# A sparse graph kernel whose gathered edge values are replaced by diagonal values, with a pass that counts them

## The chip, the cores and the metric

The kernel runs on one core of one Trainium2 chip. The metric is the device time of one execution in microseconds (us), taken without a profiler. The engines are TensorE (PE in the profile; its weight loads are PEld), VectorE (DVE), ScalarE (ACT), GpSimd (POOL) and SyncE (SP), which here only issues DMAs. Each engine works through its own queue in order, and semaphores order the engines against each other. SBUF is the memory on the chip that the engines work in, PSUM holds the sums of TensorE.

## The reference, cut to what matters

There are N = 2708 nodes with D = 128 features. `adj` is a random sparse 0/1 matrix with ones on the diagonal whose rows are divided by their sums, so all nonzero values of one row are equal, and equal to the row's diagonal element.

```python
# layer 0
XW = mobius_matvec(W, X)
gamma = 2.0 / maximum(1.0 - sum(XW * XW), EPS)
two_mean = (A_hat @ (gamma * XW)) / _clamp_abs(A_hat @ (gamma - 1.0))
...
x = layernorm(x + expmap0(relu(logmap0(AXW))))
# layer 1
s = x @ msg_w[:, :D].T
d = x @ msg_w[:, D:].T
messages = gelu(s[:, None, :] + d[None, :, :] + msg_b)
aggregated = einsum('ijd,ij->id', messages, adj)
h = gelu(concat([x, aggregated]) @ upd_w.T + upd_b) + x
x = layernorm(x + (layernorm(h) * ln_w + ln_b))
```

Layer 0 is a dense product of `adj` with a 128-column matrix. Layer 1 needs a message only where `adj[i, j]` is not zero, which is a few edges per node.

## The kernel before, in words

The nodes stand in NB = 22 blocks of 128 rows. The host hands over `adj` itself, its transpose in blocks without the diagonal (`adj_t`), and a packed array with the weights and the diagonal, `dg[:, b]` for block b.

**Layer 0.** After a setup (lines up to 310) that makes the 130 columns of `y`, the main loop walks over the blocks. `layer0(b)` loads the block's part of `adj_t` (128 × 22 × 128 float32, 1.44 MB) through SP into `aT`, which has two buffers (L317). ScalarE turns it into signs in bfloat16 (`sgn`, one buffer, L319), which also sums them per row into `signs`. TensorE multiplies it with `y` in 22 matmuls (L324), and VectorE adds the diagonal part (L328).

**Finding the edges.** From the signs, `keys` makes rows of keys on TensorE (L350), from which VectorE takes the largest eight at a time (MAX8, L358). `extract(l)` turns a list of these into tiles of 128 edges each. There are 25 lists and 99 tiles (TILES), where a tile t holds 128 edges of one block: `R[:, t, :]` says as a 0/1 matrix which row each edge belongs to (L412, L414), `J[:, t]` holds the index of the neighbour (L447), and `rid[:, t]` the number of the row (L444). They come out of matmuls with `R` (L438) and a nearest distance (L441). The address of the edge's element in `adj` is then made in `F` (L448, three buffers, one per list), and POOL fetches the value itself with an indirect DMA, one for each tile, into `V[:, t]` (the `gather` of L191). Lists found in one block are finished in the next two, interleaved with their layer-0 matmuls. The small tiles of `extract` come from a pool with two buffers per name.

**Between the layers.** `layer0_end` runs for the blocks 0–15 during the main loop and for 16–21 after it. It finishes layer 0, makes `s` (`s_nm`) and `d`, and writes `d` through SP to a table in DRAM (L535), from which the messages' gathers read.

**Layer 1.** First ScalarE applies Gelu to the sum of s and d of each node itself (L583), the message along the diagonal, and multiplies it with the diagonal (L585, 22 instructions); `own` adds it to the block's sum on TensorE (L669). Then `messages` walks over a block's tiles in quads of up to four: POOL gathers the rows d_j of 128 edges (L191), TensorE multiplies `R` with `s_nm` (L652) to lay s_i beside them, VectorE makes the weighted 0/1 matrix `rv` for the way back (L654) and adds both (L657), ScalarE applies Gelu (L658), and TensorE sums the messages per row into the PSUM tile `ag` (L660). The gathered rows go into a ring of RING = 7 quads, and later into a freed `aT` buffer, the slab. For the first EARLY = 8 blocks the edges to nodes below 16 × 128 are done ahead in a loop of their own (L687, result copied at L691); then the loop over GROUPS of blocks does the rest, copies the sum to `agT` (L702), and calls `update` (four or five matmuls and a Gelu, L606–L614) and, per group, `finish` (two layer norms and the output's DMA through SP, L616–L637). There are 35 quads in all.

**The end.** L708–L757 sum several conditions under which the lists of edges could be incomplete into one flag, among them whether the sum of the signs equals the number of edges found. The flag is read at L759; if it is set, a dense form of layer 1 follows (L760). With this input it is not.

The order in each engine's queue is made by a planner from the program's order, its dependencies and its own costs, so that instructions of neighbouring quads interleave; `issue_after` and `high_priority` bind it at the borders of the stages.

Of the kernel before, what the change touches and what calls it, by code (L numbers as in the profile page):

```python
# [31 lines left out]


SPLIT = 16
RING = 7


# [38 lines left out]
def hyperbolic_then_message_kernel(  # L76
# [4 lines left out]
    x_nm: bass.AP,  # L81
    x_t: bass.AP,
    pack: bass.AP,
    table: bass.AP,
# [22 lines left out]
    w0_sb, wT, rowvec, o = pk[:, :D], pk[:, D : 5 * D].rearrange("p (i d) -> p i d", d=D), {}, 5 * D  # L107
# [3 lines left out]
    mb, dg = pk[:, o : o + 1], pk[:, o + 1 : o + 1 + NB]  # L111
# [14 lines left out]
    ones_b = const.tile([P, P], BF16, name="ones_b")  # L126
# [39 lines left out]

    R = big.tile([P, NT, P], F32, name="R")
    J = const.tile([P, NT], U32, name="J")
    V = const.tile([P, NT], F32, name="V")
    rid = const.tile([P, NT], F32, name="rid")  # L170
    top = const.tile([P, NC], F32, name="top")
    limit = const.tile([P, NT], F32, name="limit")
# [17 lines left out]
    def gather(o, src, at):  # L190
        nc.gpsimd.indirect_dma_start(  # L191
            out=o, out_offset=None, in_=src, in_offset=bass.IndirectOffsetOnAxis(ap=at, axis=0)
        )
# [5 lines left out]
    def bank(name, bufs=2):  # L199
        return ps.tile([P, 512], F32, name=name, bufs=bufs)  # L200
# [10 lines left out]

    def cols(n):
        count[0] += 1
        return sc.tile([P, n], F32, name=f"c{count[0]}")

    def rsqrt(v, n, pool=None):

# [94 lines left out]
    ss, ssp = cols(NB), cols(NB)  # L312

    def layer0(b):

# [50 lines left out]
    def extract(l):  # L366
# [2 lines left out]
        C = wa + wb  # L369

        def tmp(name, dt=F32, w=CMAX):
            return small.tile([P, w], dt, name=name)[:, :C]

        tk = top[:, c0 : c0 + C]
        u0, u1 = 8 * (wa > 0), C - 8 * (wb > 0)
# [51 lines left out]
            )  # L427
        z = zs[l % 2][:, : C + 1]
        nc.vector.scalar_tensor_tensor(z[:, 1:], scan, SPAN, code, op0=OP.mult, op1=OP.add)
        F = small.tile([P, TMAX], U32, name="F", bufs=3)  # L430
        step = 512 // (C + 1)
        for k0 in range(0, n, step):
            k1 = min(n, k0 + step)
            w = k1 - k0
            t = slice(t0 + k0, t0 + k1)
            sp = bank("sel", 1)[:, : w * (C + 1)].rearrange("p (t c) -> p t c", t=w)
            for k in range(w):
                nc.tensor.matmul(sp[:, k, :], lhsT=R[:, t0 + k0 + k, :], rhs=z, start=True, stop=True)  # L438

            dist = small.tile([P, 512], F32, name="work", bufs=3)[:, : w * C].rearrange("p (t c) -> p t c", t=w)  # L440
            nc.vector.tensor_tensor(  # L441
                dist, sp[:, :, 1:], place[:, k0:k1].unsqueeze(2).to_broadcast([P, w, C]), op=OP.subtract
            )
# [4 lines left out]
            nc.vector.scalar_tensor_tensor(  # L448
                F[:, k0:k1], J[:, t], float(b * P * N - 1), rid[:, t], op0=OP.add, op1=OP.add
            )  # L450
        for t in range(t0, t0 + n):
            gather(V[:, t : t + 1], adj.rearrange("i (j o) -> (i j) o", o=1), F[:, t - t0 : t - t0 + 1])

    x1, x1T = x_sb, xT
    s_nm = mx
# [1 line left out]
    def layer0_end(b0, b1):  # L457

        n = b1 - b0
        sb = slice(b0, b1)  # L460

        den, r = nom[:, sb, D], nom[:, sb, D + 1]
        di, t, v, e, f = (cols(n) for _ in range(5))
# [112 lines left out]

    gd = nom
    for ins in last.values():  # L580
        ctx.enter_context(tc.issue_after(ins.ins))
    for g, n in quads:
        nc.scalar.activation(gd[:, g : g + n, :D], gd[:, g : g + n, :D], AF.Gelu)  # L583
        for k in range(n):
            nc.scalar.mul(gd[:, g + k, :D], gd[:, g + k, :D], dg[:, g + k : g + k + 1])  # L585
# [56 lines left out]
    def messages(b, ag, tiles, first, final, bins, room=ring):  # L642

        for q, k0 in enumerate(range(0, len(tiles), 4)):
            ts = tiles[k0 : k0 + 4]
            w = len(ts)
            dd = room(w)
            X = bank(bins[q % len(bins)]).rearrange("p (t d) -> p t d", d=D)[:, :w, :]
            rv = edge.tile([P, 4, P], F32, name="rv", bufs=3)
            for k, t in enumerate(ts):  # L650
                gather(dd[:, k, :], table[: SPLIT * P] if t in soon else table, J[:, t : t + 1])
                nc.tensor.matmul(X[:, k, :], lhsT=R[:, t, :], rhs=s_nm[:, b, :], start=True, stop=True)  # L652

                nc.vector.tensor_scalar(  # L654
                    rv[:, k, :], iotaN, rid[:, t : t + 1], V[:, t : t + 1], op0=OP.is_equal, op1=OP.mult
                )
            nc.vector.tensor_tensor(dd, X, dd, op=OP.add)  # L657
            nc.scalar.activation(dd, dd, AF.Gelu)  # L658
            for k in range(w):
                nc.tensor.matmul(  # L660
                    ag[:, :P],
                    lhsT=dd[:, k, :],
                    rhs=rv[:, k, :],
                    start=(first and k0 == 0 and k == 0),
                    stop=(final and k0 + k == len(tiles) - 1),
                )

    def own(b, ag):
        nc.tensor.matmul(ag[:, :P], lhsT=gd[:, b, :D], rhs=ident, start=True, stop=False)  # L669
# [6 lines left out]
        soon.update(early[b])  # L676

    slab, quads_in = stream.tile([P, NB, P], F32, name="aT"), [0, 0]

    def roomy(w):  # L680
        quads_in[0] += 1
# [65 lines left out]
    nc.vector.tensor_reduce(cnt[:, 1:2], deg.rearrange("p l k -> p (l k)"), axis=AX.X, op=OP.add)  # L747
    bp = bank("sel", 1)
    nc.tensor.matmul(bp[:, 0:2], lhsT=ones, rhs=flags, start=True, stop=True)
    nc.tensor.matmul(bp[:, 2:4], lhsT=ones, rhs=cnt, start=True, stop=True)  # L750
    tot = sc.tile([P, 4], F32, name="tot")
    nc.scalar.copy(tot, bp[:, 0:4])
    nc.vector.tensor_tensor(tot[:, 2:3], tot[:, 2:3], tot[:, 3:4], op=OP.not_equal)
    nc.vector.tensor_add(tot[:, 0:1], tot[:, 0:1], tot[:, 1:2])
    nc.vector.tensor_add(tot[:, 0:1], tot[:, 0:1], tot[:, 2:3])
    flag = sc.tile([P, 1], I32, name="flag")
    nc.vector.tensor_copy(flag, tot[:, 0:1])  # L757

    dense = nc.values_load(flag[0:1, 0:1], min_val=0, max_val=2 * P + 1)  # L759
# [35 lines left out]
]  # L795


def by_partition(a, w):

    n = a.shape[0]  # L800
    nb = (n + P - 1) // P
    whole = np.zeros((nb * P, w), a.dtype)
    whole[:n] = a.reshape(n, w)
    return whole.reshape(nb, P, w).transpose(1, 0, 2).reshape(P, nb * w)


def layouts(x, adj, w0, msg_w, msg_b, upd_w, upd_b, ln_w, ln_b):

    n = adj.shape[0]
    nb = (n + P - 1) // P  # L810
    whole = np.zeros((nb * P, nb * P), adj.dtype)
    whole[:n, :n] = adj
    np.fill_diagonal(whole, 0.0)
    t = whole.reshape(nb, P, nb, P).transpose(0, 3, 2, 1)
# [4 lines left out]
    parts += [msg_b.reshape(P, 1), by_partition(np.diagonal(adj), 1)]  # L819
    return {  # L820
        "adj_t": np.ascontiguousarray(t),
        "x_nm": by_partition(x, P),
        "x_t": xt,
        "pack": np.ascontiguousarray(np.concatenate(parts, axis=1)),
    }


# [31 lines left out]
```

## Time and profile before

| | |
|---|---|
| median of 3 runs | 389.42 us (389.2 to 390.23) |
| the profiled execution | 504.16 us |
| its span | 502.5 us |
| mean clock granted to TensorE in it | 0.783 |
| setup, up to the first matmul of L324 | 0 to 30.5 us |
| main loop, up to the last matmul of L324 | 30.5 to 268.3 us |
| first matrices `rv` of layer 1 | 338.8 us |
| last gather of values (L191 into `V`) starts | 306.7 us |
| last matrix `rv` of layer 1 starts | 463.4 us |

The profile is one execution taken by the hardware profiler, and it was longer than the runs that give the median. In the page, one line per engine gives its busy time, its share of the span and its instructions. The rows of 40 digits cut the span in 40 equal slices of 12.6 us, with the busy share of a slice in tenths. The chain line gives the shares of the chain of work that ended last. A row of a group has the line, engine and operation, then the tile written and the tiles read, their shapes, the number of instructions, the busy time and the mean in nanoseconds, and at last the idle time of the engine just ahead of them with what ended most of it. In a table by stage every engine has its busy microseconds and in brackets the number of its instructions, and PEclk is the granted clock. A line of waits has who waited for whom, then the total in us, the number of waits and the longest. "remote" and "issue" are waits whose releaser the profile does not show.

### The profile page before, as it was taken

The numbers are of one execution on the slowest core, as the hardware profiler recorded it, in microseconds if no ns is written. First come the engines' busy times: TensorE is split into PE (matmuls) and PEld (weight loads), VectorE is DVE, ScalarE is ACT, GpSimd is POOL, SyncE is SP. The second block draws the span as 40 slices with busy tenths as digits, with TensorE's granted clock in tenths as the row PEclk, the third lists the DMA queues.
The fourth block names the chain that finished last, engine by engine and source line by source line (L and its number), as shares of the span: only waits on it lengthen the run. The fifth ranks groups of instructions, "written<-read, shape, count | busy, mean of one in ns | idle before, by whom it ended". The sixth has DMA issues, their size and how long they took to land.

```text
span 502.5 us, 7784 instructions
## 1 busy us (share of the span) xinstructions
PE 333.5 (66%) x2427; PEld 297.2 (59%) x2427; DVE 275.9 (55%) x1474; ACT 208.0 (41%) x562; POOL 203.5 (40%) x297
## 2 busy tenths in 40 slices
PE   4269788674899989797973111538397697679620
PEld 4269677564889878795862001338395576557410
DVE  2979546433666565798740067248272226376671
ACT  2827325432657465794650022135032112326521
POOL 5301454571644525222257707722616572470000
PEclk9759779885999999998995555657679557798855
DMA  8306322223345544433421101110201120111100
GB/s 341 167 2 232 115 84 79 88 98 116 118 132 214 193 156 164 184 117 115 137 80 37 52 7 31 52 53 15 49 12 37 42 54 17 38 42 48 32 23 20
DMA packets 16237, 45.14 MB, mean 90 GB/s; under 512 B 5626, under 2 KB 11150, under 8 KB 13374
## 3 DMA queue, kind: packets, MB, share of 16 engines
q1 hardware_dynamic: 9710, 37.43, 20.6%
q0 software_dynamic: 6336, 6.55, 5.4%
q10 hardware_dynamic: 144, 0.60, 0.4%
q8 instruction: 20, 0.33, 0.3%
q14 instruction: 27, 0.22, 0.1%
HBM read 41.74 MB, written 2.83 MB: 89 GB/s over the span
## 4 chain that ended last, share of the span: by engine, by line
PE 32%; DVE 21%; issue 16%; another core or an unknown queue 14%; ACT 10%; DMA 4%; POOL 1%; DVEq 0%; POOLq 0%; ACTq 0%; SPq 0%
PE mp L324 7%; PE X L652 4%; PE mp L660 4%; PE kx L350 4%; PE sel L438 3%; DVE top L358 2%; ACT nom L635 2%; ACT sgn L319 2%; PE ag L660 2%; PE sel L612 1%; PE sel L613 1%; PE sel L610 1%; DMA xT<-in_x_t_dram 1%; DMA V<-in_adj_dram,F 1%
## 5 line engine op out<-in xcount | busy, mean ns | idle before, releaser
L191 POOL DMA_INDIRECT V<-in_adj_dram,F x99 | 94.9, 959 | 156.2 <-DVE top L358 31.0
L324 PE MATMUL mp<-y,aT 128*128 128x130 f32 x968 | 129.2, 288 | 1.4 <-DVE y L308 0.9
L324 PEld LDWEIGHTS mp<-y,aT 128*128 128x128 f32 x968 | 120.1, 199 | 2.3 <-DVE y L308 1.1
L191 POOL DMA_INDIRECT dd<-table_dram,J x81 | 78.1, 965 | 83.7 <-ACT agT L702 21.7
L319 ACT ACTIVATE sgn<-aT 128x2816 bf16<-128x2816 f32 x22 | 56.1, 2548 | 24.5 <-issue 20.5
L350 PE MATMUL kx<-kd,sgn 128*128 128x128 bf16 x484 | 41.5, 240 | 26.6 <-issue 19.1
L350 PEld LDWEIGHTS <-sgn 128*128 128x128 bf16 x484 | 33.3, 108 | 40.1 <-issue 31.4
L652 PE MATMUL X<-mx,R 128*128 128x128 f32 x198 | 41.1, 357 | 16.9 <-DVE dd L657 6.9
L654 DVE TENSOR_SCALAR rv<-iotaN,rid,V 128x128 f32<-128x128 f32 x99 | 30.1, 351 | 32.6 <-remote 20.0
L652 PEld LDWEIGHTS X<-mx,R 128*128 128x128 f32 x198 | 36.2, 265 | 19.2 <-DVE dd L657 7.5
L438 PE MATMUL sel<-z,R 128*128 128x49 f32 (+4 forms) x198 | 31.4, 299 | 23.3 <-DVE R L414 9.6
L438 PEld LDWEIGHTS sel<-z,R 128*128 128x128 f32 x198 | 28.3, 213 | 25.8 <-DVE R L414 10.4
L358 DVE MAX8 top<-kx 128x8 f32<-128x128 f32 (+3 forms) x152 | 28.6, 236 | 19.9 <-remote 14.8
L441 DVE TENSOR_TENSOR work<-sel,place 128x144 f32<-128x144 f32 (+11 forms) x29 | 11.7, 403 | 40.5 <-remote 30.9
L409 ACT ACTIVATE work<-iota,mid 128x512 f32<-128x512 f32 (+3 forms) x53 | 26.8, 553 | 5.5 <-DVE mid L402 5.4
L657 DVE TENSOR_TENSOR dd<-X,dd 128x384 f32<-128x384 f32 (+3 forms) x29 | 15.2, 526 | 21.7 <-remote 7.5
L444 ACT COPY rid<-sel 128x3 f32<-128x3 f32 (+5 forms) x29 | 4.7, 162 | 46.0 <-DVE work L441 36.3
L660 PE MATMUL mp<-rv,dd 128*128 128x128 f32 x116 | 21.6, 321 | 3.1 <-ACT dd L658 3.1
L402 DVE SCALAR_TENSOR_TENSOR mid<-sel,deg 128x2 f32<-128x2 f32 x25 | 3.9, 155 | 35.7 <-ACT oe L399 35.7
L610 PE MATMUL sel<-pk,xT 128*128 128x128 f32 x44 | 12.6, 377 | 16.4 <-ACT nom L614 10.4
L658 ACT ACTIVATE dd<-dd 128x384 f32<-128x384 f32 (+3 forms) x29 | 13.7, 497 | 20.3 <-DVE dd L657 14.5
L399 ACT COPY oe<-sel 128x2 f32<-128x2 f32 x25 | 4.0, 159 | 43.2 <-PE kx L350 25.9
(204 smaller groups left out, 614.6 us busy)
## 6 DMA issues: line engine op xcount, KB each, us to landing
aT<-in_adj_t_dram SPq DMA_DIRECT2D x22, 1408.0 KB, 6.7
V<-in_adj_dram,F POOLq DMA_INDIRECT x99
xT<-in_x_t_dram SPq DMA_DIRECT2D x2, 704.0 KB
x_sb<-in_x_nm_dram SPq DMA_DIRECT2D x2, 704.0 KB
out_dram<-nom SPq DMA_DIRECT2D x21, 64.0 KB, 1.6
dd<-table_dram,J POOLq DMA_INDIRECT x81
table_dram<-dt SPq DMA_DIRECT2D x5, 256.0 KB
pk<-in_pack_dram ACTq DMA_DIRECT2D x1, 587.5 KB
```

Of the source, the lines that this page charges most:

```text
L191: nc.gpsimd.indirect_dma_start(out=o, out_offset=None, in_=src, in_offset=bass.IndirectOffsetOnAxis(ap=at, axis=0))
L319: nc.scalar.activation(sgn, aT, AF.Sign, accum_out=signs[:, b : b + 1])
L324: nc.tensor.matmul(op[:, : D + 2], lhsT=aT[:, j, :], rhs=y[:, j, :], start=(j == 0), stop=(j == NB - 1))
L350: nc.tensor.matmul(kp[:, i * P : (i + 1) * P], lhsT=sgn[:, j, :], rhs=kd[:, q, :], start=False, stop=(i == len(groups) - 1 and j == j1 - 1),)
L358: nc.vector.max(top[:, c : c + 8], seg[:, s, :])
L409: nc.scalar.activation(r0, iota[:, k0 * P : k1 * P], AF.Abs, scale=2.0, bias=mid[:, k : k + 1])
L438: nc.tensor.matmul(sp[:, k, :], lhsT=R[:, t0 + k0 + k, :], rhs=z, start=True, stop=True)
L610: nc.tensor.matmul(up[:, :D], lhsT=x1T[:, s], rhs=wT[:, 2, :], start=True, stop=False)
L652: nc.tensor.matmul(X[:, k, :], lhsT=R[:, t, :], rhs=s_nm[:, b, :], start=True, stop=True)
L654: nc.vector.tensor_scalar(rv[:, k, :], iotaN, rid[:, t : t + 1], V[:, t : t + 1], op0=OP.is_equal, op1=OP.mult)
L657: nc.vector.tensor_tensor(dd, X, dd, op=OP.add)
L660: nc.tensor.matmul(ag[:, :P], lhsT=dd[:, k, :], rhs=rv[:, k, :], start=(first and k0 == 0 and k == 0), stop=(final and k0 + k == len(tiles ...
```

## The change

The tiles `V` and `F` go, with the 99 gathers of values. Instead, layer 1 takes the edges of a row with weight one and multiplies the sum per row with the diagonal element of the row: the 22 multiplications of L585 go, `rv` becomes a plain comparison of `iotaN` with `rid` (one instruction per run of consecutive tiles), and `scaled` puts a product with the diagonal, laid along the columns by a DMA of 64 KB per block, where the sum was copied (8 copies of L691 and 22 of L702).

That the diagonal element is the value of every edge of its row is tested along with it. `fetch` loads the rows of `adj` in 44 halves (128 × 1354 float32) through SP into the second `aT` buffer, which layer 0 no longer needs. `count_on`, called after each quad, compares one or two halves with the diagonal on VectorE (result in bfloat16, in the buffer of `sgn`) and sums the hits per column on TensorE in three matmuls into a PSUM bank that collects over all halves, `hits`. Two halves are loaded ahead, and each comparison is followed by the load of the half after the next. At the end the total of `hits` less N is compared with the sum of the signs, and the lowest diagonal element with zero; both go into the flag.

To make room, the small tiles of `extract` other than `m` and `whole` get one buffer instead of two, and columns in `sc` share names. The sums of the early blocks move from the bank `ag` to `mp`, which has two buffers.

```diff
+FOURS = 34
...
-    V = const.tile([P, NT], F32, name="V")
...
         def tmp(name, dt=F32, w=CMAX):
-            return small.tile([P, w], dt, name=name)[:, :C]
+            return small.tile([P, w], dt, name=name, bufs=2 if name in ("m", "whole") else 1)[:, :C]
...
-        F = small.tile([P, TMAX], U32, name="F", bufs=3)
...
-            nc.vector.scalar_tensor_tensor(
-                F[:, k0:k1], J[:, t], float(b * P * N - 1), rid[:, t], op0=OP.add, op1=OP.add
-            )
-        for t in range(t0, t0 + n):
-            gather(V[:, t : t + 1], adj.rearrange("i (j o) -> (i j) o", o=1), F[:, t - t0 : t - t0 + 1])
...
         nc.scalar.activation(gd[:, g : g + n, :D], gd[:, g : g + n, :D], AF.Gelu)
-        for k in range(n):
-            nc.scalar.mul(gd[:, g + k, :D], gd[:, g + k, :D], dg[:, g + k : g + k + 1])
...
-                nc.vector.tensor_scalar(
-                    rv[:, k, :], iotaN, rid[:, t : t + 1], V[:, t : t + 1], op0=OP.is_equal, op1=OP.mult
+            k = 0
+            while k < w:
+                n = next((i for i in range(1, w - k) if ts[k + i] != ts[k] + i), w - k)
+                nc.vector.tensor_tensor(
+                    rv[:, k : k + n, :],
+                    iotaN.unsqueeze(1).to_broadcast([P, n, P]),
+                    rid[:, ts[k] : ts[k] + n].unsqueeze(2).to_broadcast([P, n, P]),
+                    op=OP.is_equal,
                 )
+                k += n
...
+            count_on()
+
+    def scaled(o, b, ag):
+
+        v = edge.tile([P, P], F32, name="v")
+        nc.scalar.dma_start(v, diag[:, b * P : (b + 1) * P].to_broadcast([P, P]))
+        nc.vector.tensor_mul(o, ag[:, :P], v)
+
+
+    halves = [(b, h) for b in range(NB) for h in range(2)]
+    walked = [0, 0]
+
+    def fetch(k):
+        b, h = halves[k]
+        a = beside[: rows[b], h * (N // 2) : (h + 1) * (N // 2)]
+        nc.sync.dma_start(a, adj[b * P : b * P + rows[b], h * (N // 2) : (h + 1) * (N // 2)])
+        return a
+
+    def count_on():
+
+        walked[0] += 1
+        while walked[1] < min(len(halves), walked[0] * len(halves) // FOURS):
+            k = walked[1]
+            b, h = halves[k]
+            eq = stream.tile([P, NB, P], BF16, name="sgn", bufs=1).rearrange("p j i -> p (j i)")[: rows[b], : N // 2]
+            nc.vector.tensor_scalar(eq, fetched[k], dg[: rows[b], b : b + 1], None, op0=OP.is_equal)
+            for c0 in range(0, N // 2, 512):
+                c1 = min(N // 2, c0 + 512)
+                nc.tensor.matmul(
+                    hits[:, : c1 - c0], lhsT=ones_b[: rows[b], :], rhs=eq[:, c0:c1],
+                    start=(k == 0 and c0 == 0), stop=(k == len(halves) - 1 and c1 == N // 2),
+                )
+            if k + 2 < len(halves):
+                fetched.append(fetch(k + 2))
+            walked[1] += 1
...
     slab, quads_in = stream.tile([P, NB, P], F32, name="aT"), [0, 0]
+    beside = stream.tile([P, NB, P], F32, name="aT").rearrange("p j i -> p (j i)")
+    hits = bank("ag", 1)
+    fetched = [fetch(0), fetch(1)]
...
     for b in range(EARLY):
-        ag = bank("ag", 1)
+        ag = bank("mp")
         own(b, ag)
         messages(b, ag, early[b], False, True, ["X"], roomy)
-        nc.scalar.copy(gd[:, b, :D], ag[:, :P])
+        scaled(gd[:, b, :D], b, ag)
...
-            nc.scalar.copy(agT, ag[:, :P])
+            scaled(agT, b, ag)
             update(h, b - g0, b, [agT, gd[:, b, :D]] if b < EARLY else [agT])
...
+    nc.vector.tensor_reduce(low, dg, axis=AX.X, op=OP.min)
+    nc.vector.scalar_tensor_tensor(flags[:, 1:2], low, 0.0, flags[:, 1:2], op0=OP.is_le, op1=OP.add)
...
+    nc.vector.tensor_reduce(tot[:, 4:5], hits, axis=AX.X, op=OP.add)
+    nc.vector.tensor_scalar_add(tot[:, 4:5], tot[:, 4:5], -float(N))
```

The host also hands over the diagonal as one row (`diag`), with ones where the last block is padded.

More of the change, by code (lines that the diff above doesn't have):

```diff
@@ L83, in hyperbolic_then_message_kernel @@
     pack: bass.AP,
+    diag: bass.AP,
     table: bass.AP,
@@ L213, in cols @@
         count[0] += 1
-        return sc.tile([P, n], F32, name=f"c{count[0]}")
+        return sc.tile([P, NB], F32, name=f"c{count[0]}")[:, :n]
     def rsqrt(v, n, pool=None):
@@ L310, in hyperbolic_then_message_kernel @@
         )
-    ss, ssp = cols(NB), cols(NB)
+    ss, ssp = (sc.tile([P, NB], F32, name=name) for name in ("ss", "ssp"))
     def layer0(b):
@@ L460, in layer0_end @@
         sb = slice(b0, b1)
+        count[0] = 0
         den, r = nom[:, sb, D], nom[:, sb, D + 1]
@@ L747, in hyperbolic_then_message_kernel @@
     nc.vector.tensor_reduce(cnt[:, 1:2], deg.rearrange("p l k -> p (l k)"), axis=AX.X, op=OP.add)
+    low = sc.tile([P, 1], F32, name="lowest")
+    nc.vector.tensor_reduce(low, dg, axis=AX.X, op=OP.min)
+    nc.vector.scalar_tensor_tensor(flags[:, 1:2], low, 0.0, flags[:, 1:2], op0=OP.is_le, op1=OP.add)
     bp = bank("sel", 1)
@@ L750, in hyperbolic_then_message_kernel @@
     nc.tensor.matmul(bp[:, 2:4], lhsT=ones, rhs=cnt, start=True, stop=True)
[L751 to L755, printed above, removed]
+    tot = sc.tile([P, 5], F32, name="tot")
+    nc.scalar.copy(tot[:, :4], bp[:, 0:4])
+    nc.vector.tensor_reduce(tot[:, 4:5], hits, axis=AX.X, op=OP.add)
+    nc.vector.tensor_scalar_add(tot[:, 4:5], tot[:, 4:5], -float(N))
+    nc.vector.tensor_tensor(
+        tot[:, 3:5], tot[:, 3:5], tot[:, 2:3].to_broadcast([P, 2]), op=OP.not_equal
+    )
+    for k in (1, 3, 4):
+        nc.vector.tensor_add(tot[:, 0:1], tot[:, 0:1], tot[:, k : k + 1])
     flag = sc.tile([P, 1], I32, name="flag")
     nc.vector.tensor_copy(flag, tot[:, 0:1])
-    dense = nc.values_load(flag[0:1, 0:1], min_val=0, max_val=2 * P + 1)
+    dense = nc.values_load(flag[0:1, 0:1], min_val=0, max_val=3 * P + 2)
     with tc.If(dense > 0):
@@ L795, with by_partition @@
 ]
-def by_partition(a, w):
+def by_partition(a, w, pad=0.0):
     n = a.shape[0]
     nb = (n + P - 1) // P
-    whole = np.zeros((nb * P, w), a.dtype)
+    whole = np.full((nb * P, w), pad, a.dtype)
     whole[:n] = a.reshape(n, w)
@@ L818, in layouts @@
     parts += [np.broadcast_to(v, (P, P)) for v in (upd_b, ln_w, ln_b, msg_b)]
-    parts += [msg_b.reshape(P, 1), by_partition(np.diagonal(adj), 1)]
+    parts += [msg_b.reshape(P, 1), by_partition(np.diagonal(adj), 1, 1.0)]
+    diag = np.ones((1, nb * P), adj.dtype)
+    diag[0, :n] = np.diagonal(adj)
     return {
@@ L824, in layouts @@
         "pack": np.ascontiguousarray(np.concatenate(parts, axis=1)),
+        "diag": diag,
     }
```

## The prediction, made before the change was run

> **What bounds the kernel now.** I read the page first, then the time by stage, then the waits, then the timeline of the start of layer 1.
>
> ```profile
> span 502.5 us, 7784 instructions
> PE 333.5 (66%) x2427; PEld 297.2 (59%) x2427; DVE 275.9 (55%) x1474; ACT 208.0 (41%) x562; POOL 203.5 (40%) x297
> PE   4269788674899989797973111538397697679620
> POOL 5301454571644525222257707722616572470000
> PE 32%; DVE 21%; issue 16%; another core or an unknown queue 14%; ACT 10%; DMA 4%; POOL 1%; DVEq 0%; POOLq 0%; ACTq 0%; SPq 0%
> ```
>
> No engine is the bound over the whole span. The profiled execution took 504.16 us and its span is 502.5, while the unprofiled median is 389.42. So 115 us of the profile are not in the time that is measured, and every stall has to be asked whether it exists without the profiler. I form the sum of the differences against the profiled execution and carry it over to 389.4 only where its mechanism does not need the profiler's stalls.
>
> ```profile
> core 0: us, PE busy (x) PEld busy (x) DVE busy (x) ACT busy (x) POOL busy (x), PEclk, DMA share, GB/s
> 151.00:202.00 51.00, 47.71 (x474) 44.88 (x473) 30.55 (x180) 30.14 (x72) 21.85 (x23) 1.00 0.52 186
> 270.00:300.00 30.00, 4.43 (x20) 2.06 (x18) 6.69 (x58) 3.33 (x12) 14.16 (x15) 0.50 0.11 31
> 338.00:403.00 65.00, 46.09 (x262) 42.06 (x263) 32.38 (x123) 20.11 (x58) 29.09 (x31) 0.71 0.12 31
> 403.00:466.00 63.00, 50.03 (x271) 42.56 (x270) 31.87 (x142) 20.68 (x60) 27.35 (x28) 0.77 0.15 39
> ```
>
> The table by stage says more. At 151–202 us layer 0 is bound by TensorE: busy 47.7 of 51 us at full clock, six blocks in 51 us, while POOL's 23 instructions, nearly all of them gathers, run beside it. There a gather costs nothing visible. Layer 1 (338–466 us) has TensorE busy 96 of 128 us, VectorE 64, POOL 56, and the DMA engines nearly idle. It is a loop of short dependent steps, with VectorE's adds and ScalarE's Gelus between two groups of matmuls.
>
> ```profile
> DVE work L441 <- remote: 30.9, 8, 7.3
> POOL V L191 <- DVE F L448: 30.2, 7, 9.5
> DVE rv L654 <- remote: 20.0, 4, 6.8
> SPq L317 <- PE mp L324: 167.4, 16, 34.2
> ...
> L191 POOL DMA_INDIRECT V<-in_adj_dram,F x99 | 94.9, 959 | 156.2 <-DVE top L358 31.0
> L654 DVE TENSOR_SCALAR rv<-iotaN,rid,V 128x128 f32<-128x128 f32 x99 | 30.1, 351 | 32.6 <-remote 20.0
> ```
>
> The largest row of POOL is the 99 gathers that go away. But POOL waits for VectorE there (L448), not VectorE for POOL. L441 has no wait on a gather in the code, only on matmuls. The values V are read first at L654, after 338 us, when the last of them (306.7 us) has long landed.
>
> **What the Trainium skill says.** "VectorE: DVE Perf Modes", The perf-mode tier table: a float32 tensor_scalar in SBUF runs at two elements a cycle, a float32 tensor_tensor at one, anything with PSUM at one. The trace agrees: L414 takes 278, 349, 418 and 516 ns for 128, 256, 384 and 512 columns, about 75 ns per 128; L657 with its PSUM operand takes 287 to 689 ns. "DMA: Bandwidth & Descriptors", Anatomy of one DMA: some 2 us fixed (measured there on POOL's path), plus bytes over the bandwidth. SP's loads of aT agree in kind: one that ran alone was issued at 118.24 us and moved from 119.0 to 123.4. The same page, Issuing engines are not separate DMA queues: transfers of SP, ACT and POOL share the 16 engines, so the new loads and the gathers of layer 1 meet; no row of before shows how much that costs.
>
> **The change, part by part.**
>
> 1. *Gathers of V and F.* 99 × (0.96 + 0.30 us of issue) = 125 us of POOL go from layer 0, and 29 × 0.16 = 4.6 us of F from VectorE. The cover is the TensorE-bound stretch. A list can wait for the gathers of the list three before it, since F has three buffers, and the first two blocks bring 28 gathers (35 us of POOL) within two blocks of 8 us. I take 4 us gained. Bounds: 0, and about 40 (six blocks between 46 and 135 us took 89 us where TensorE's own work is 48) if those stalls come from the gathers and exist unprofiled. The layer-1 gathers stay; the early ones were done before 338 us, so POOL brings layer 1 no earlier.
>
> 2. *ScalarE's 22 multiplications (L585).*
>
> ```profile
> 338.93 2.43 ACT L585 ACTIVATE nom<-nom,pk 128x128 f32<-128x128 f32 x8
> 342.09 1.85 ACT L585 ACTIVATE nom<-nom,pk 128x128 f32<-128x128 f32 x6
> 343.84 2.38 ACT L658 ACTIVATE dd<-dd 128x512 f32<-128x512 f32 x5
> 344.55 4.80 PE L660 MATMUL ag<-rv,dd 128*128 128x128 f32 x34
> 347.18 0.97 POOL L191 DMA_INDIRECT dd<-table_dram,J  x1 [16.54 <-PE ag L660]
> ```
>
> They stand on ScalarE just ahead of the first Gelu of messages, whose sum matmuls free the ring for POOL. 22 × 0.305 = 6.7 us go. Up to 6 us come forward, if nothing new limits the first quads.
>
> 3. *rv.* 99 × 0.351 = 34.7 us of execution (30.1 us busy, overlaps counted once) become about 38 instructions over the same columns at one element a cycle: 38 × 0.15 + 99 × 0.134 = 19 us (fixed part and rate from L657's 287 ns for 128 columns and 689 for 512; 17 to 25). VectorE gains some 9 us (5 to 13) where overlapped starts are allowed for.
>
> 4. *scaled().* 30 ScalarE copies of 0.26 us become 30 VectorE products from PSUM at 0.29 us (row of L657 with 128 columns): +8.7 us VectorE, −7.8 ScalarE. 30 DMAs of 64 KB join ACT's queue. An output of that size lands in 1.6 us; with two buffers it is prefetched two blocks ahead, so it costs nothing unless ACT's queue is late. Bounds −1 and +15 us (0.5 us for each of 30). I take 0.
>
> 5. *Row loads and compares.* 44 halves of 128 × 1354 float32, 0.69 MB, 29.3 MB in all. One compare: 516 + (842 / 128) × 75 = 1.0 us, extrapolated from L414 (lower 0.9, upper 1.6 if the bfloat16 output takes it to one element a cycle). 44 of them: 44 us more for VectorE. The loop is closed: load k+2 is issued only when compare k has ended. A half moves in 0.69 / 1.44 × 4.4 = 2.1 us (the lone aT load); with the other 1.5 to 2.5 us between issue and landing, it lands about 4 us after its issue. Two buffers take turns: 4.0 + 1.0 compare + 0.4 in VectorE's order and for semaphores = 5.4 us for two halves, 2.7 us each. After the two prefetched ones 42 × 2.7 = 113 us, plus some 5 us for the first two and the last: layer 1 cannot be shorter than 118 us. In the profiled execution it is 128 and the loop just fits. What is it unprofiled? From 389.4 I take 30.5 for setup, 22 blocks × 8 = 176 (TensorE's 47.7 / 6), 10 for the last keys, 34 for layer 0's end (45 in the profile without the 11.2 us that PE waits there for "issue") and 36 for the tail: 103 us for layer 1, an estimate. Layer 1 then grows by 118 − 103 = +15 us, and the 6 us of part 2 and the 9 of part 3 vanish, because the loads and not ScalarE or VectorE's rv decide. Bounds: 0 (all hidden) and +40.
>
> 6. *Matmuls of counts.* 132 bfloat16 matmuls, at 0.38 us each (L344, 512 columns) 50 us at most, at full clock nearer 0.25, so 33. TensorE has 32 us idle in the profiled layer 1. They queue behind their compare, and the next X matmuls behind them. Inside the 118 us this fits if the clock stays up; bounds 0 and +25. I take 0 on top of part 5.
>
> 7. *Buffers.* extract's small tiles with one buffer order VectorE against ScalarE and TensorE within a list: 0 to +6 us, beside the TensorE-bound blocks; I take 1. The double bank for early sums: 0 to −2. The end: the flag now follows the last half, asked one quad before the end, so the 36 us tail covers it; six tiny instructions of 0.2 us, +1.
>
> Sum: −4 + 15 + 0 + 0 + 1 + 1 = +13, less about 1 for the second bank: +12. Profiled, 504 − 4 to −40 from layer 0 and 0 to +12 in layer 1: some 495, although the median rises. The median: 389.4 + 12 = 401.
>
> **The rivals.**
>
> *Forecast: the closed loop of loads sets layer 1*, 401 us, own range 392 to 412. For it: loads of 1.44 MB take 6.7 us from issue to landing, and only two halves are in flight. Against it: the profiled layer 1 is slow enough to hide it.
>
> *A, the other side: everything new is hidden* and the gains stay. Place: VectorE's 64 idle us and the idle DMA engines of layer 1. Price: −4 (part 1) − 6 (part 2) and +1 = about 380 us; 355 to 388 if more of layer 0's stalls were the gathers' doing. It decides if a half costs less than 103 / 44 = 2.3 us a cycle, that is, if it lands within 3.3 us of its issue. Against it: layer 1's steps are dependent and each compare stands in order before some add.
>
> *B: VectorE and TensorE in order become the bound.* VectorE: 64 + 44 + 9 − 9 = 108 us, TensorE 96 + 33 to 50 = 129 to 146 at the profiled clocks, with every wait between them kept: layer 1 at 103 + 35 = 138, minus the gains: 389.4 − 4 + 35 = 420; range 412 to 440. For it: a compare that waits for its load blocks the rv and adds behind it, and so POOL's ring. Against it: a busier TensorE gets a higher clock (0.71 and 0.77 in layer 1, 1.00 in the dense blocks).
>
> *C: gains and costs cancel*, 389: half of part 5 against parts 1 and 2.
>
> **How the numbers follow.** Forecast 0.42, A 0.27, B 0.25, C 0.06. Time 401. Leaving out the far ends of A and B, the range is 372 to 428. A measurement of this kernel can tell about 0.3% (1.2 us) from no change. Faster: A and half of what C has outside that bound, 0.29. Same: 0.04. Slower: 0.67.
>
> **What would show it.** Right: layer 1 at 115 us or more; the compares of count_on waiting for their row loads, at a regular spacing of 2.5 to 3 us; VectorE's compare near 1.0 us; 250 GB/s through layer 1. Layer 0's cadence unchanged at 8 us where TensorE is busy. Wrong: compares that never wait for a DMA (then A or B), a layer 0 that is tens of microseconds shorter without the profiler, TensorE busy over 90% of layer 1 (B), or products of scaled() that wait for their 64 KB rows.

## The result, and the profile after

| | before | after |
|---|---|---|
| median, same sessions | 389.83 us (389.2 to 390.6, 4 runs) | 424.39 us (421.92 to 427.92, 4 runs) |
| ratio | | 1.0892, 95% interval 1.0798 to 1.0987 |
| profiled span | 502.5 us | 420.1 us |

The change made the kernel 35 us slower. For all that follows one thing must be known: the kernel before takes about 390 us in some sessions and about 498 us in others, and this is not bound to the chip (two chips showed both), and its profile above is from one of the second kind, so each group of runs below is read against its own runs of before. I call them the 390 and the 498 condition. The profile after is from the 390 condition, so the two spans are not to be subtracted. Where single runs of a group lie over 1.5% above the fastest of the same kernel, the medians below are of the others.

The page of the changed kernel, its span, two lines of slices (40 of 10.5 us) and the chain by engine and by line:

```profile
span 420.1 us, 7958 instructions
PE 325.4 (77%) x2547; PEld 281.1 (67%) x2559; DVE 308.0 (73%) x1460; ACT 195.8 (47%) x510; POOL 119.0 (28%) x198
PE   3339999999999999979992076778877969778430
POOL 6400000000000000000067777772777776000000
...
PE 54%; DVE 20%; DMA 17%; ACT 3%; issue 3%; POOL 1%; DVEq 0%; ACTq 0%
PE mp L325 25%; DMA aT<-in_adj_dram 8%; PE kx L351 6%; PE sel L438 6%; DMA v<-in_diag_dram 6%; DVE sgn L694 3%; PE ag L697 3%; PE X L524 3%; PE mp L662 3%; PE kx L345 2%; DMA pk<-in_pack_dram 1%; PE X L647 1%; DVE work L279 1%; DVE top L359 1%; PE sel L607 1%
...
aT<-in_adj_dram SPq DMA_DIRECT2D x42, 677.0 KB, 5.4
v<-in_diag_dram ACTq DMA_DIRECT2D x30, 64.0 KB, 4.2
```

DMA is 17% of the chain, 14 of these 17 for the row loads and the diagonal's loads. The 4% in the profile before can't stand beside it: in the 498 condition the changed kernel's own profile (after_again, below) gives 6% to DMA and 9% to an unknown queue. In the 390 condition the kernel without the counting pass (no_counts_v8, below) has 5%. A half lands 5.4 us after its issue, a diagonal row of 64 KB 4.2 us after (medians of the 16 and 19 loads whose landing the profile has). The table by stage shows where the time goes:

```profile
254.00:300.00 46.00, 36.82 (x255) 30.71 (x260) 36.09 (x99) 9.09 (x19) 30.51 (x27) 0.96 0.82 259
300.00:357.00 57.00, 47.94 (x282) 37.92 (x288) 40.98 (x126) 12.35 (x34) 43.63 (x40) 0.88 0.82 258
357.00:390.00 33.00, 26.02 (x137) 18.69 (x138) 24.99 (x100) 13.89 (x37) 0.03 (x1) 0.83 0.72 216
```

The columns are PE, PEld, DVE, ACT and POOL busy, the granted clock, the share of the DMA engines and GB/s. In layer 1 the DMA engines are now 82% busy up to 357 us and 72% after, and neither TensorE (36.8 of 46 us at 254–300) nor VectorE (36.1) is full. The chain of waits between 261 and 275 us tells what the kernel waits for there (start, duration, piece):

```profile
261.36 0.91 DVE sgn L694
...
262.29 5.48 DMA aT<-in_adj_dram
...
267.86 0.94 DVE sgn L694
...
268.81 5.36 DMA aT<-in_adj_dram
...
274.29 0.94 DVE sgn L694
```

A compare ends, SP issues the load of the half after next 0.03 us later (median of 42), that load takes 5.4 us, and here the next compare of that buffer starts at once. This is the closed loop. Its 44 compares start between 255.2 and 405.4 us, one every 3.49 us, so one buffer comes round every 7.0 us: 5.9 us from the issue of a load to its compare, 0.93 for the compare and 0.13 to the next issue (means of 42). The kernel ends 15 us after the start of the last compare.

VectorE stands idle ahead of a compare for its load for only 11.3 us in all, in 14 waits. The larger wait is on TensorE, in whose queue three count matmuls follow each compare:

```profile
L697 PE MATMUL ag<-sgn,ones_b 128*128 128x512 bf16 (+3 forms) x120 | 38.8, 418 | 25.7 <-DVE sgn L694 24.7
```

TensorE is idle for 24.7 us ahead of count matmuls that wait for their compare, and no matmul behind them in its queue runs meanwhile.

### The profile page after: what moved, and what is told of

Same layout as the page of the kernel before. It is cut to its first block, busy times and chain, and to the rows that moved or that the text cites. A ratio compares the mean times of both kernels' runs of the same rounds, so it can differ in the third digit from the quotient of the medians.

```text
span 420.1 us, 7958 instructions
## 1 busy us (share of the span) xinstructions
PE 325.4 (77%) x2547; PEld 281.1 (67%) x2559; DVE 308.0 (73%) x1460; ACT 195.8 (47%) x510; POOL 119.0 (28%) x198
## 4 chain that ended last, share of the span: by engine, by line
PE 54%; DVE 20%; DMA 17%; ACT 3%; issue 3%; POOL 1%; DVEq 0%; ACTq 0%
PE mp L325 25%; DMA aT<-in_adj_dram 8%; PE kx L351 6%; PE sel L438 6%; DMA v<-in_diag_dram 6%; DVE sgn L694 3%; PE ag L697 3%; PE X L524 3%; PE mp L662 3%; PE kx L345 2%; DMA pk<-in_pack_dram 1%; PE X L647 1%; DVE work L279 1%; DVE top L359 1%; PE sel L607 1%
## 5 line engine op out<-in xcount | busy, mean ns | idle before, releaser
L192 POOL DMA_INDIRECT dd<-table_dram,J x81 | 86.5, 1068 | 228.7 <-DVE junk_p L335 195.5
L697 PE MATMUL ag<-sgn,ones_b 128*128 128x512 bf16 (+3 forms) x120 | 38.8, 418 | 25.7 <-DVE sgn L694 24.7
L694 DVE TENSOR_SCALAR sgn<-aT,pk 128x1354 bf16<-128x1354 f32 (+1 forms) x44 | 41.0, 932 | 14.8 <-DMA aT<-in_adj_dram 11.3
L351 PE MATMUL kx<-kd,sgn 128*128 128x128 bf16 x484 | 33.7, 222 | 7.5 <-ACT sgn L320 7.5
L697 PEld LDWEIGHTS <-ones_b 128*128 128x128 bf16 (+1 forms) x132 | 14.1, 109 | 37.8 <-issue 33.2
L647 PE MATMUL X<-mx,R 128*128 128x128 f32 x198 | 31.3, 285 | 7.4 <-DVE dd L659 5.4
L647 PEld LDWEIGHTS X<-mx,R 128*128 128x128 f32 x198 | 26.6, 196 | 10.9 <-DVE dd L659 6.7
L359 DVE MAX8 top<-kx 128x8 f32<-128x128 f32 (+3 forms) x152 | 28.4, 235 | 2.7 <-PE kx L351 2.7
L662 PEld LDWEIGHTS mp<-rv,dd 128*128 128x128 f32 x162 | 24.7, 219 | 4.8 <-ACT dd L660 1.9
L192 POOL DMA_INDIRECT aT<-table_dram,J x18 | 19.6, 1089 | 5.5 <-issue 3.7
L652 DVE TENSOR_TENSOR rv<-iotaN,rid 128x384 f32<-128x384 f32 (+3 forms) x35 | 18.2, 528 | 0.0
```

The lines of the kernel that those rows point to most:

```text
L192: nc.gpsimd.indirect_dma_start(out=o, out_offset=None, in_=src, in_offset=bass.IndirectOffsetOnAxis(ap=at, axis=0))
L351: nc.tensor.matmul(kp[:, i * P : (i + 1) * P], lhsT=sgn[:, j, :], rhs=kd[:, q, :], start=False, stop=(i == len(groups) - 1 and j == j1 - 1),)
L359: nc.vector.max(top[:, c : c + 8], seg[:, s, :])
L652: nc.vector.tensor_tensor(rv[:, k : k + n, :], iotaN.unsqueeze(1).to_broadcast([P, n, P]), rid[:, ts[k] : ts[k] + n].unsqueeze(2).to_broad ...
L662: nc.tensor.matmul(ag[:, :P], lhsT=dd[:, k, :], rhs=rv[:, k, :], start=(first and k0 == 0 and k == 0), stop=(final and k0 + k == len(tiles ...
L694: nc.vector.tensor_scalar(eq, fetched[k], dg[: rows[b], b : b + 1], None, op0=OP.is_equal)
```

## The experiments

The theories as they stood: L, the closed loop of row loads sets layer 1; D, the compares and count matmuls in order on VectorE and TensorE do; S, the product with the diagonal waits for its own load; G, in the 498 condition the gathers stall the other engines. All times are medians, with the ratio to the runs of before in the same group and its 95% interval.

### The 498 condition

**before_again**, no edit.

> The kernel before once more, for a second profile, because the first was 115 us longer than the median. All theories: time 389 to 391 us. If the stalls of the first profile were the profiler's alone, its span now may come near 389 us, with layer 1 (first rv to last) near 100 us and a main loop of 22 blocks near 8 us each. If the gathers of values really stall layer 0, the blocks between the second and the eighth take more than 10 us each here too.

It took 495.41 us, in one run, beside 497.9: the 502.5 us of the first profile were no mishap of the profiler but this condition. Here is one row of it, the matmuls of layer 0 (minimum/median/maximum of one in ns, then first and last start):

```profile
L324 PE MATMUL mp<-y,aT x968: 272/275/587, 30.5 to 258.4; 128*128 128x130 f32 x194
```

**no_V_gather** and **no_V_gather_2**, the kernel before without the gathers of values:

```diff
+    nc.gpsimd.memset(V, 1.0)
...
-        for t in range(t0, t0 + n):
-            gather(V[:, t : t + 1], adj.rearrange("i (j o) -> (i j) o", o=1), F[:, t - t0 : t - t0 + 1])
```

> The kernel before with the 99 gathers of values left out and V set to one, so the edge values are left out of its result; all else stays. Where before takes 390 us: G is not at work and my step 1 expects 4 us less (386), at most 40 less. Where before takes 498 us: G expects 455 to 465 us.

> The kernel before without the 99 gathers of values and with V set to one. Where before takes 390 us: step 1 of my forecast says 4 us less, 386, bounds 350 to 390; theory G (the gathers stall the other engines only in the other condition) 386 to 390. Where before takes 498: 469 again.

468.6 us beside 497.0 (0.9443, 0.9376 to 0.951) and 464.71 beside 497.62 (0.9338, 0.929 to 0.9386): 28 and 33 us. The same row, in no_V_gather:

```profile
L325 PE MATMUL mp<-y,aT x968: 272/275/585, 30.5 to 219.0; 128*128 128x130 f32 x194
```

Layer 0 ends at 219.0 instead of 258.4 us with matmuls of the same 275 ns. So in this condition the gathers do stall it. G holds here, for some 30 of the 108 us between the two conditions. How the gathers of values do alone in the 390 condition was not measured.

**no_counts** and **no_counts_2**, the changed kernel without fetch and count_on:

```diff
-            count_on()
...
-    hits = bank("ag", 1)
-    fetched = [fetch(0), fetch(1)]
```

> Leaves out the loads of adj's rows, the compares and the count matmuls; the flag keeps its other terms. Theory L (the closed loop of row loads, two in flight, 3 us a half, sets layer 1) and theory D (44 compares and 132 matmuls in order on VectorE and TensorE set it): 380 to 392 us, so that the counts carry all of the +35. Theory S (the product with the diagonal waits for its own 64 KB load, 4 to 6 us after the product before): stays at 400 to 412 us.

> Loads, compares and count matmuls left out, as in the earlier run. Where before takes 390 us: L and D 380 to 392 us, S (the product with the diagonal waits for its own load) 400 to 412. Where before takes 498 us: 461 us again.

460.97 us beside 497.9 (0.9273, 0.921 to 0.9336), and 465.09 beside 497.0 (0.935, 0.9223 to 0.9477). One line of no_counts shows what the stall is like:

```profile
270.56 0.30 DVE L359 MAX8 top<-kx 128x8 f32<-128x128 f32 x1 [40.50 <-remote]
```

The MAX8 reads matmuls whose last recorded ones run at 223 us; it starts at 270.6, 6.5 us after the last of some 40 gathers in a row (264.0). In the changed kernel's profile of the 390 condition the first MAX8 of this block starts at 220.4, while the gathers run on. In its profile of the 498 condition (after_again) the same MAX8 starts at 271.0, and the first compare of the count at 305.5 instead of 255.2 us: some 50 of the 64 us between these two profiles of one kernel (484.4 and 420.1 us) arise at this place. That the layer-1 gathers, brought ahead to 212 us, stall the end of layer 0 there is read from these times; no run took these gathers away. Why the MAX8 starts so late was not found.

**same_rows** (compares and sums over the first two halves, no more loads) and **loads_only** (all loads, compares of two columns):

```diff
-                fetched.append(fetch(k + 2))
+                fetched.append(fetched[k])
```

```diff
-            nc.vector.tensor_scalar(eq, fetched[k], dg[: rows[b], b : b + 1], None, op0=OP.is_equal)
-            for c0 in range(0, N // 2, 512):
+            nc.vector.tensor_scalar(eq[:, :2], fetched[k][:, :2], dg[: rows[b], b : b + 1], None, op0=OP.is_equal)
+            for c0, c1 in [(0, 2)]:
```

> Compares and sums as in the changed kernel, but always over the two halves loaded first: 42 row loads left out, the count is of the wrong rows and is left out of the flag. L: the loads were the price, so 390 to 402 us. D: stays at 418 to 426. S: between, 405 to 415, because the diagonal's loads get faster when the row loads are gone.

> All 44 row loads in the same closed loop, but each compare reads two columns only and one tiny matmul follows it: nearly all work of the compares and sums is left out. L: 44 times about 2.7 us remain, so 405 to 418 us. D: 385 to 395 us. S: 400 to 415, with the waits for the diagonal's loads as long as in the changed kernel.

469.97 us (0.9458, 0.9392 to 0.9524) and 478.4 (0.9638, 0.9564 to 0.9712), both beside 497.9. Against 460.97 for neither, the work of counting costs 9 us alone and the loads 17 alone.

**after_again**, and **v8** with **v8_2**, the changed kernel with eight buffers for the diagonal's rows:

```diff
-        v = edge.tile([P, P], F32, name="v")
+        v = edge.tile([P, P], F32, name="v", bufs=8)
```

> The changed kernel once more, as the reference of this group of runs. Where the kernel before takes about 390 us, all theories expect 422 to 428 us. Where it takes about 498 us, because TensorE hardly advances while POOL issues gathers (theory G: 99 fewer gathers in layer 0 are worth some 35 us there), 480 to 495 us, faster than before; theories L and D without G expect +35 us there too, 533 us.

> The changed kernel with eight buffers instead of two for the diagonal row v of scaled(), so that its 64 KB loads can be issued up to eight blocks ahead. S: the 25 us that these loads hold on the chain of waits go, so 15 to 25 us below the changed kernel in the same group. L and D: within 5 us of it.

> The changed kernel with eight buffers for the diagonal row v. Where before takes 390 us (the changed kernel 424, without counts and with these buffers 387): S expects 400 to 412, L and D at least 418. Where before takes 498: 475 again.

The changed kernel takes 485.72 us beside 497.0 (0.9798, 0.9708 to 0.9887): in the 498 condition it is 2% faster. Within this group the 11 us divide into 28.4 less without the gathers of values (no_V_gather), 3.5 less for the rest of the edits (no_counts_2), and 20.6 more for counting. v8 takes 474.4 beside the same 497.0 (0.9534, 0.9393 to 0.9676), 11 below the changed kernel; v8_2, in another group, 479.83 beside 497.62 (0.963, 0.9564 to 0.9695), which is 6.5 us further below its kernel before than after_again is below its own. So S has a part, of 6 to 11 us, where I had 0. In the 390 condition v8 alone was not measured; in the changed kernel's profile there VectorE waits 10.3 us in all for rows v.

**loads_only_v8** and **same_rows_v8** (the edits of loads_only and same_rows with eight buffers for v), and the same kernels as loads_only_v8_b, same_rows_v8_b and loads_only_v8_c:

> Eight buffers for v, all row loads in their closed loop, but compares of two columns and one tiny matmul each; the other work of counting is left out. Where before takes 390 us: L 408 to 416, D 387 to 393. Where before takes 498: L 472, D 462.

> Eight buffers for v, all compares and count matmuls, but over the two halves loaded first; the other 42 row loads are left out, and the count from the flag. Where before takes 390 us: D 408 to 416, L 387 to 395. Where before takes 498: D 472, L 465.

> As loads_only_v8: the row loads' closed loop without the work of counting. Where before takes 390 us: L 408 to 416, D 387 to 393. Where before takes 498: 474 again.

> As same_rows_v8: the work of counting without 42 of the row loads. Where before takes 390 us: D 408 to 416, L 387 to 395; 397 to 405 in both runs would say that the two prices add up. Where before takes 498: 473 again.

> As loads_only_v8, row loads without the work of counting. Where before takes 390 us: if the closed loop of loads is a floor of its own (44 times 2.7 to 3 us), 408 to 416; if loads and compares only together make the price (a compare that waits holds up VectorE's queue), 390 to 402. Where before takes 498: 475 again.

Loads alone: 474.0, 477.04 and 477.45 us (0.9531, 0.9577, 0.9541). Counting work alone: 472.6 and 472.66 us (0.9481, 0.9466). Here the two cost about the same, and they don't separate the theories: each theory came within 6 us for the part that it blames (472 for both), and neither low figure came (D 462 for the loads, L 465 for the counting work). So in this condition both parts have a price. These five runs are inconclusive for the 390 condition.

### The 390 condition

**no_counts_v8**, without counting and with eight buffers for v:

> Eight buffers for the diagonal row v, and the loads, compares and count matmuls left out: what remains if both suspects are gone. Where before takes about 498 us: S alone (v's loads are late in their own right) expects 450 to 456 us, 10 below the run without counts; if v's loads are late only because they share the DMA engines with the row loads, 461 to 466, as without v8. Where before takes 390 us: 375 to 386 us.

387.0 us beside 389.67, ratio 0.9928 (0.9907 to 0.9948). So without counting and with eight buffers for v the whole of the loss is gone, and all other edits together gain 2.7 us. Its stages and its gathers (number, then busy time in us and mean in ns):

```profile
254.00:300.00 46.00, 44.05 (x335) 40.87 (x336) 33.52 (x116) 13.24 (x31) 35.11 (x36) 0.96 0.35 83
300.00:339.00 39.00, 30.01 (x186) 26.39 (x184) 22.18 (x96) 12.98 (x35) 30.03 (x30) 0.87 0.32 75
```

```profile
L192 POOL DMA_INDIRECT dd<-table_dram,J x81 | 79.1, 976 | 220.0 <-DVE near L446 195.6 <-issue 18.6 <-DMA dd<-table_dram,J 1.2
```

POOL runs through: 99 gathers from 212.3 to 339 us, one every 1.28 us, with a gap of 0.3 us ahead of each and none longer. VectorE's adds wait 12.5 us in all for gathered rows, in six waits, and POOL with its gathers' landing is 24% of the chain between 255 and 360 us. So the train of layer-1 gathers is what paces this kernel after TensorE's first 46 us (busy 44.05).

**same_rows_v8_c**, the edit of same_rows with eight buffers for v:

> As same_rows_v8. Where before takes 390 us: D 408 to 416, L 387 to 395; 397 to 405 would say that loads and compares share the price. Where before takes 498: 473 again, and nothing new.

396.93 us beside 390.57, ratio 1.0165 (1.0106 to 1.0224): 10 us over no_counts_v8, between L and D, at the lower edge of the stretch that was to mean "both". Its stages and its count matmuls:

```profile
254.00:300.00 46.00, 43.14 (x295) 35.43 (x301) 44.02 (x113) 10.81 (x24) 36.94 (x30) 0.96 0.29 71
300.00:353.00 53.00, 48.40 (x329) 38.97 (x335) 47.19 (x150) 18.54 (x49) 41.95 (x37) 1.00 0.27 68
```

```profile
L697 PE MATMUL ag<-sgn,ones_b 128*128 128x512 bf16 (+3 forms) x121 | 32.6, 359 | 1.0 <-issue 0.2
```

TensorE and VectorE are each busy 91 of 99 us, and the compares wait 5.3 us in all for the count matmuls ahead of them, which read the one buffer of `sgn`. This is D's mechanism, two queues in order that are nearly full. TensorE's wait ahead of the count matmuls, 24.7 us in the changed kernel, is gone with the row loads. POOL is changed too:

```profile
L192 POOL DMA_INDIRECT dd<-table_dram,J x81 | 92.1, 1137 | 220.4 <-DVE near L446 196.0 <-issue 16.1 <-PE mp L662 1.5
```

The mean gather is 1137 ns instead of 976, with no row load in the queue after the first two. The timelines of POOL and of the compare show where the longer ones lie:

```profile
302.86 1.59 POOL L192 DMA_INDIRECT dd<-table_dram,J  x1 [0.30 <-issue]
304.75 1.53 POOL L192 DMA_INDIRECT dd<-table_dram,J  x1 [0.30 <-issue]
306.58 0.94 POOL L192 DMA_INDIRECT dd<-table_dram,J  x1 [0.30 <-PE mp L662]
```

```profile
302.71 0.92 DVE L694 TENSOR_SCALAR sgn<-aT,pk 128x1354 bf16<-128x1354 f32 x1
305.24 0.92 DVE L694 TENSOR_SCALAR sgn<-aT,pk 128x1354 bf16<-128x1354 f32 x1
307.59 0.93 DVE L694 TENSOR_SCALAR sgn<-aT,pk 128x1354 bf16<-128x1354 f32 x1 [0.42 <-PE ag L697]
```

Here the gathers that meet a compare take 1.5 to 1.6 us, the one between two compares 0.94. Over all 99, the 53 that overlap a compare take 1.26 us on average (0.94 to 1.78), the other 46 take 0.97; in the changed kernel it is 1.23 and 0.97. The Trainium skill, "DMA: Bandwidth & Descriptors", SWDGE vs HWDGE vs iDMA, says that VectorE in its 2-port mode locks GpSimd out of the SBUF state that it writes when it generates descriptors. The compare (0.93 us for 1354 columns) is near the two-element slope of L414, and the trace agrees in kind; that this lock is the reason was not tested by a run of its own. 81 × 0.16 us = 13 us of POOL, and the last gather starts at 352.8 instead of 338.0 us.

POOL is therefore a third full queue here, but the trace doesn't put the 10 us on it: no add of VectorE waits for a gathered row, where six did in no_counts_v8, and POOL has 0% of the chain, beside 63% for TensorE and 23% for VectorE. Which of the three would have to be relieved first was not tested.

**early_v8**, eight buffers, and 12 halves counted behind layer 0's end, the other 32 over the quads:

```diff
+AHEAD = 12
...
     with tc.high_priority():
         for _ in layer0_end(*CHUNKS[-1]):
             pass
+    count_on(AHEAD)
```

> The changed kernel with eight buffers for v and with the first 12 halves counted behind the last chunk of layer 0's end instead of in layer 1 (the other 32 over the 34 quads). L: 12 times 3 us leave layer 1, so about 25 us below v8 where layer 0's end has room: 455 to 465 us where before takes 498, 385 to 400 where it takes 390. D: about 12 us below v8, as VectorE's and TensorE's work moves too.

414.8 us beside 389.67, ratio 1.0639 (1.0596 to 1.0682), worse than the 385 to 400 that L expected. A quarter of the loop moved out of layer 1 together with eight buffers for v is worth some 10 us, not 25. Its profile (417.8 us) shows why. The last compare starts at 383.1 instead of 405.4 us: the loop ends 22 us earlier, near what L said. But the last Gelu of `update` starts at 392.8 us, after 388.8 in the changed kernel and 359.0 in no_counts_v8, so the quads between the compares came no sooner. L's time per half describes the loop and not the whole kernel. That the 32 remaining loads still hold up the queues of VectorE and TensorE between the quads fits this (TensorE waits 33.4 us in all ahead of count matmuls for their compares here), but was not tested. With eight buffers for v and all 44 loads, this run is also 18 us over same_rows_v8_c; so most of what comes with the loads is not due to v's two buffers, as far as the other place of 12 halves allows the comparison. No run here beats the kernel before in the 390 condition while it keeps the count.

## Why the prediction was right or wrong

The direction was right, the size was not: +12 us foretold, +35 measured.

- **Part 5, the step that failed.** The forecast put a half's landing at 4.0 us and the loop at 5.4 us for two halves, from a load of aT that ran alone. Measured under its own traffic: 5.4 us from issue to landing (median), 5.9 to the compare (mean), and 2 × 3.49 = 7.0 us for two halves. The loop takes 150 us (255.2 to 405.4) where I had 118. The compare itself (0.93 us, 1.0 foretold) and layer 1 without the loop (103 us estimated; in no_counts_v8 it runs from the first rv at 253.8 to the last Gelu of `update` at 359.0, 105 us) were right. The mis-sized term was the landing time: I gave each half the DMA engines alone, while the loop itself keeps two halves in flight. The same lone load (5.7 us from issue to landing, 4.4 of them moving) would have given 2 × 2.1 + 1.3 = 5.5 us for two halves that share the engines, an estimate. The first two halves, issued together at about 210 us ahead of v's rows, fit it: one landed in 4.5 us in the changed kernel, one in 5.8 us in same_rows_v8_c. What the gathers and v's rows add was not separated.
- **Two errors in part made up for each other.** With 150 in place of 118, the forecast's own sum gives 433 us, more than the 424 measured, although the loop also begins 5 us later than the sum has it (255.2, not 250.5). What makes up for it is the tail: the sum has 36 us behind the loop, and only 15 follow the start of the last compare, because most of the last groups' work runs beside the loop (the last Gelu of `update` starts at 388.8).
- **The split of the +37** between no_counts_v8 and the changed kernel: 10 us is the counting work without its loads, the other 27 come with the loads, v's two buffers among them. That loads alone make these 27 is not shown, since neither loads_only nor v8 met the 390 condition. The loop in the trace, TensorE's wait ahead of the count matmuls (24.7 us; 33.4 with the loads and eight buffers for v in early_v8; at most 1.0 without the loads), and the 18 us of early_v8 speak for it.
- **Part 6**, 0 us on top, bounds 0 and +25: 10 us. I had counted 32 us of idle TensorE in layer 1, from a profile of the 498 condition; in same_rows_v8_c TensorE and VectorE have 8 us left of 99. A count matmul took 0.36 us on average there and 0.42 in the changed kernel, beside L344's 0.38. That the gathers on POOL would stretch was not foreseen.
- **Part 1**, 4 us, bounds 0 and 40. In the 390 condition all edits but the counting gain 2.7 us net, with eight buffers for v, and the gathers' own share is not known; in the 498 condition, from which the profile was, some 30 for the gathers. The bounds were right, and so was the choice to credit little of the profile's stalls. That "those stalls come from the gathers" was the truth about the profile; that they were "the profiler's" was not. The forecast for a profiled run, some 495 us, belonged to that condition: after_again has 484.4.
- **Parts 2 and 3**, 6 and 9 us if nothing limits the first quads. No load limits no_counts_v8 and they still do not appear: POOL's train does. rv fell from 30.1 to 18.2 us busy, as worked out. My reading that POOL had waited for TensorE at 347 us came from the 498 condition.
- **Part 4**, 0 us: 6 to 11 in the 498 condition. An output's 1.6 us was the wrong row for v, which lands in 3.0 us without the row loads (no_counts_v8) and 4.2 us beside them, and two buffers tie each load to the product two blocks before.
- **Rival B** had 420 us and almost hit the number, which is in part luck: in the changed kernel TensorE is less busy in layer 1 than without counting (36.8 against 44.05 of 46 us), not over 90%. Its mechanism, full queues on TensorE and VectorE, is what the counting work does without its loads, for 10 us. What it said of a compare that waits for its load and holds up what stands behind it is seen on TensorE. **Rival A** fell: a half takes 3.49 us, not 2.3. **C** fell with the +35.

## What to carry to other kernels

A stream of loads that each wait for the use of the one two before is a closed loop, and its floor is (landing + use) / buffers × loads, with the landing time taken under the traffic that the change itself brings, the loop's other loads first: here (5.4 + 0.93) / 2 × 44 = 139 of the 150 us. The floor of the loop is not the time of the kernel: with a quarter of it moved away, 22 us less of loop were 10 us less of kernel. Before a stall in a profile is credited, compare the profile's span with the unprofiled median; where they differ by a quarter, as here, the profile may show another condition of the same program. And ask of every engine with a low share whether it runs without gaps in the stage that counts: without the counting pass POOL was busy 28% of the span and yet paced layer 1.

## What the runs showed of the hardware

- The same program took 390 or 498 us by session, on the same chips. In the slower condition a MAX8 on VectorE started 47 us after the last recorded matmul that it reads, while POOL issued some 40 gathers back to back; 40.5 us of this are a wait whose releaser the profile doesn't show. In the faster one it started within 1 us, with the same gathers running. Layer 0's matmuls take their 275 ns in both.
- POOL gathers that overlap a VectorE compare of 128 × 1354 float32 take 1.26 us on average (53 of them, up to 1.78) instead of 0.97 (same_rows_v8_c).
- A 64 KB load that repeats one row over 128 partitions lands in 3.0 us (no_counts_v8), and in 4.2 us beside the row loads, where an output of 64 KB took 1.6 us before.
- With two loads of 677 KB in flight, and gathers and 64 KB loads beside them, a load lands in 5.4 us (median) and the DMA engines move 258 GB/s, 82% busy.
